# Two graph layers with attention in between: when VectorE takes statistics and squares, and when x is asked for

## Chip, cores and metric

The kernel runs on one core of a Trainium2 chip. The metric is the device time of one execution in microseconds (us); lower is better.

## What is computed

x has 16 graphs of 1024 nodes and 256 channels; adj is a sparse 1024 x 1024 matrix. Everything is 32-bit floating point. Cut to what matters:

```python
# layer 0, h = relu(layernorm(x))
c     = mean(h, channels)                        # one number per node and graph
A     = 2*abs(abs(sigmoid(c[:,None,:]-c[:,:,None]) - 0.5) - 0.5)
q     = relu((h^T @ (adj * sym(A))) * para)      # per graph, weights differ by graph
k, v  = h @ kv_w
x     = x + softmax(q k^T * scale) v             # 4 heads of 64
# layer 1, h = relu(layernorm(x)), A_hat = normalized adj, the same for all graphs
agg   = A_hat @ h                                # aggregate
y     = agg @ W1^T + b1                          # 512 columns, "hidden"
h1    = relu(batchnorm(y))                       # statistics over all graphs and nodes
out   = batchnorm(h1 @ W2^T + b2)
x     = x + out
```

The batch norm over all graphs is why the hidden results y are written to DRAM, with their statistics collected on the way, and read again in a second pass.

## The kernel before

**Layout.** A graph is held as 8 tiles of 128 nodes. The products of 1024 x 1024 with 1024 x 256 (queries and aggregate) and the hidden product use a seven-product scheme on halves, so that each has seven products whose sums are made on VectorE. All products go through three PSUM banks that rotate, `ps_mm` with the tag "mm" (`bank`, `product`, L174): a product can start when the result that lay in its bank three banks ago has been taken out.

**Two streams woven by hand.** The program's order on each engine is the order in which Python emits it. `attention` runs over 16 graphs x 16 steps. A step issues a pair of score tiles (`scores`, matmul L1056, exponential on ScalarE L1064), sums of exponentials on VectorE (L1085, L1088), and the values of the step before (L1099). Between them it takes pieces from a generator, `background(b)`, until the pieces' costs (their products' TensorE time) have caught up with what is due. So a step of attention alternates with two to five pieces of other work for neighbouring graphs. `weave(main, (start, side), ...)` takes from `start` on one piece of a side for each piece of `main`, and empties the sides at the end. `soon(action)` puts an action behind the next piece.

**The background of graph b** (from 1 on): four pieces of keys and values for b+1 with parts of the weights (`weigh`: ScalarE L506, L514, VectorE L493, adj loads L192); the queries of b+1 (`queries`, 14 pieces, VectorE L569 and L577 to L603, para loads L549); the first aht loads of the aggregate; x of b+2 (`load_x`, L186); the other keys and values with the norm of layer 1 for b-1. Then the aggregate of b-1 (`aggregate`, 14 pieces of 1.71 us of TensorE, aht loads L714, evictions L730 to L756, steps L786 to L788), and the hidden product of b-1 (`hidden`, 14 pieces of 0.86).

**Beside the aggregate** stands `summed(b+2)`: the norm of x for layer 0 (`Norm`: statistics L344 and L346 on VectorE, rsqrt on GpSimd L96/L97, L357 on VectorE, relu with row sums on ScalarE L368) in eight pieces, then `differences(b+2)`: the row sums turned (L465), written to DRAM (L467) and read back as a broadcast tile cbc (L471), which L506 needs.

**Beside the hidden product** stands `prepare(b+2)`. After two pieces it calls `squares` (two 32 x 32 block transposes of 128 x 1024 each, L438, then one write of 1 MB from GpSimd's queue, L442), and `gathered` reads the result back in another order as the transposed h (L450), which the keys need. The tile of the squares comes from the two buffers tagged "h", which x of the next graphs and the normalized h of layer 1 use too.

**The hidden product** per graph: seven products for each of two column blocks c, in the order shown in `hidden`; ten y tiles from `py` (tag "y", 6 buffers). `put` writes a finished y to DRAM (L824, GpSimd's queue) and takes its statistics (L825), one piece later: eight per graph. L831, L837, L842, L847, L851, L860 and L866 take the products out of their banks; L856 and L869 are GpSimd sums.

**Once, in the background of graph 0**: `plain_queries(1)` (16 pieces) with the norm of graph 2, `graph` (the combinations aht of the adjacency, GpSimd) and `degrees` (its row and column sums; ScalarE L241, VectorE L243/L244). `load_later` in the background of graph 1 loads W1, makes its sums on GpSimd (L309 to L312), writes dinv to DRAM (L314) and reads it back as a broadcast (L315).

SyncE's queue holds all loads, in program order; a load that waits holds up those behind it.

Of the kernel before, what the change touches and what calls it, by code (L numbers as in the profile page):

```python
# [10 lines left out]
F32 = mybir.dt.float32  # L11
# [6 lines left out]
P = 128  # L18
# [5 lines left out]
def gnn_two_layers_kernel(  # L24
# [12 lines left out]
    nc = tc.nc  # L37
# [3 lines left out]
    CC = C // P  # L41
# [57 lines left out]
    def layers(shifted):  # L99
# [10 lines left out]
        p2 = st.enter_context(tc.tile_pool(name=f"p2_{kind}", bufs=2))  # L110
        p3 = st.enter_context(tc.tile_pool(name=f"p3_{kind}", bufs=3))
        p8 = st.enter_context(tc.tile_pool(name=f"p8_{kind}", bufs=8))
        py = st.enter_context(tc.tile_pool(name=f"py_{kind}", bufs=6))

        p4 = attn.enter_context(tc.tile_pool(name=f"p4_{kind}", bufs=4, side="right"))
        ps_sc = attn.enter_context(
# [14 lines left out]
        def soon(action):  # L131

            queue.append(action)
# [298 lines left out]
        def squares(b):  # L432

            sq = p2.tile([P, CC, N], F32, tag="h", name=f"sq_{b}")
            for k in range(CC):
                nc.vector.transpose(  # L438
                    sq[:, k].rearrange("p (i t s) -> p i t s", i=NS, s=SQ),
                    hs["a", b][:, :, k * P : (k + 1) * P].rearrange("p t (i s) -> p i t s", s=SQ),  # L440
                )
            nc.gpsimd.dma_start(out=hsq_d[b], in_=sq)  # L442

        def gathered(b, k):

# [349 lines left out]
        def hidden(b):  # L795

            if b >= B - 2:
                yield from plain_hidden(b)
                return
            HH = H1 // 2  # L800
            a11, a12, _, a22 = w1_quarters()
            s1, s2, s3, s4 = (later["s"][:, i] for i in range(4))
            b11, t3, b21, b22 = at_quarters(b)
            t1, t2 = steps[b]
            t4 = p2.tile([P, FB], F32, tag="para", name=f"at4_{b}")
            nc.gpsimd.tensor_sub(t4, b21, t2)

            def left(block, c):
                return block[:, c * P : (c + 1) * P]

            def one(name, block, c, right):
                part = bank(f"py_{b}_{c}_{name}")
                product(part, left(block, c), right, True, True)
                return part

            made = {}

            def new(name, c):
                made[name] = py.tile([P, FB], F32, tag="y", name=f"y_{b}_{c}_{name}")
                return made[name]  # L820

            def put(y, n, j):
                i = b * NH + n
                nc.gpsimd.dma_start(out=y1_d[i][:, j, :], in_=y)  # L824
                soon(lambda: nc.vector.bn_stats(stats1[:, j, i, :], y))  # L825

            add = nc.vector.tensor_add

            def m1(c):
                part = one("1", a11, c, b11)  # L830
                nc.scalar.activation(  # L831
                    new("11", c), part, AF.Identity, bias=b1[:, c : c + 1]
                )

            def m2(c):
                y = made["11"]
                add(y, one("2", a12, c, b21), y)  # L837
                put(y, 0, c)

            def m3(c):  # L840
                y = made["12"]
                add(y, one("3", s4, c, b22), y)  # L842
                put(y, 1, c)

            def m4(c):
                y = made["21"]
                add(y, one("4", a22, c, t4), made["sum"])  # L847
                put(y, 0, 2 + c)

            def m5(c):  # L850
                nc.scalar.copy(new("22", c), one("5", s1, c, t1))  # L851
                if c == 1:
                    both(c)

            def both(c):
                nc.gpsimd.tensor_add(new("12", c), made["21"], made["22"])  # L856

            def m6(c):
                y = new("21", c)
                add(y, one("6", s2, c, t2), made["11"])  # L860
                if c == 0:
                    both(c)

            def m7(c):
                part, y = one("7", s3, c, t3), made["22"]
                nc.vector.scalar_tensor_tensor(  # L866
                    new("sum", c), part, b1_step[:, c : c + 1], made["21"], op0=ALU.add, op1=ALU.add
                )
                nc.gpsimd.tensor_add(y, y, made["sum"])  # L869
                put(y, 1, 2 + c)  # L870

            for c, order in ((0, (m1, m5, m6, m2, m3, m7, m4)), (1, (m1, m6, m2, m5, m7, m3, m4))):
                for each in order:
                    each(c)
                    yield 0.86

        def plain_hidden(b):

# [47 lines left out]
        def summed(b):  # L926
            yield from Norm(b, True).all()
            differences(b)
            yield 0.0

        def prepare(b, products):


            w = weighers[b]
            yield from islice(products, 1)
            yield from islice(products, 1)
            squares(b)
            yield from weave(islice(products, 5), (0, islice(w, 2)))
            gathered(b, 0)
            yield from weave(islice(products, 3), (0, islice(w, 1)))  # L940
            gathered(b, 1)
            yield from weave(islice(products, 3), (0, islice(w, AHEAD - 3)))
            yield from products
# [3 lines left out]
        def background(b):  # L947

            if b == 0:
                differences(1)  # L950
                for k in range(CC):
                    yield TOP
                    transposed(1, (k,))
                    yield 1.0
                w, products, norm = weighers[1], keys_values(1), Norm(2, True).all()
                yield from weave(islice(products, 4), (0, double(islice(w, 8))))
                yield from weave(
                    plain_queries(1), (0, w), (4, norm), (5, graph()), (7, degrees())
                )
                differences(2)  # L960
                w = weighers[2]
                yield from islice(products, 1)
                yield from weave(islice(products, 2), (0, islice(w, 2)))
                yield TOP
                transposed(2, (0,))
                yield 1.0
                yield from weave(islice(products, 1), (0, islice(w, 1)))
                yield from islice(w, 1)
                yield TOP
                transposed(2, (1,))  # L970
                yield 1.0
                yield from islice(w, AHEAD - 4)
                yield from products
                return
            before = hidden(b - 1)
            gather = aggregate(b - 1)
            if b + 1 < B:
                w, products, norm = weighers[b + 1], keys_values(b + 1), normed(b - 1)
                yield from weave(islice(products, 4), (0, islice(w, 4)))
                if b == 1:  # L980
                    load_later()
                yield from weave(queries(b + 1), (0, double(w)), (9, islice(norm, 5)))
                yield next(gather)
                if b + 2 < B:
                    load_x(b + 2, True)
                yield from weave(products, (0, norm))
            else:
                yield next(gather)
                yield from weave(endings.pop(), (2, normed(b - 1)))
            if b + 2 < B:  # L990
                yield from weave(gather, (3, summed(b + 2)))
                yield from prepare(b + 2, before)
            elif b + 2 == B:

                yield from gather
                endings.append(before)
            else:
                yield from gather
                yield from weave(before, (0, normed_last()))

        def shifted_attention(b):
# [285 lines left out]
        with st:  # L1287
            if shifted:
                for b in range(B):
                    if b > 0:  # L1290
                        load_x(b)
                    run(Norm(b, True).all())
                    differences(b)
                    for k in range(CC):
                        transposed(b, (k,))
                    run(islice(weighers[b], AHEAD))
                    run(weave(plain_queries(b), (0, weighers[b])))
                    if b == 0:
                        run(degrees(), graph())
                        load_later()  # L1300
                    run(keys_values(b))
                    shifted_attention(b)
                    norm = Norm(b, False)
                    run(norm.all())
                    keep(b)
                    if b == B - 1:
                        attn.close()
                        turns.append(second(kind))
                    run(aggregate(b), hidden(b))
            else:  # L1310
                idle = bank("idle")

# [375 lines left out]
```

## Time and profile before

| | |
|---|---|
| median of 3 runs | 2480.53 us (2480.22 to 2481.03) |
| the profiled execution | 2482.2 us, span 2480.3 us, mean granted clock 0.992 |
| TensorE matmul busy | 2418.3 us, 97% |
| VectorE busy | 1999.8 us, 81% |
| ScalarE busy | 1261.2 us, 51% |
| GpSimd busy | 565.2 us, 23% |
| period of a graph | about 135.5 us |
| L825 statistics | 112 of 687 ns |
| L438 squares | 26 of 1220 ns |

The profile names engines PE (TensorE; PEld is its weight load), DVE (VectorE), ACT (ScalarE), POOL (GpSimd) and SP (SyncE). A timeline row has the start, the duration, engine, line, operation, output and inputs, and in brackets the engine's idle time just before it with what ended it. A row of a table of stages has the stage, its length and the busy time of PE, PEld, DVE, ACT and POOL with the number of instructions, then the granted clock, the DMA share and GB/s. Since matmuls overlap in the array, busy TensorE is not TensorE at its pace: compare starts.

### The profile page before, as it was taken

To read this page: it belongs to the slowest core of one execution; us is meant where nothing else is said; L and a number is where in the kernel's file an instruction comes from. 1 tells how busy PE (TensorE), PEld (TensorE's weight loads), DVE (VectorE), ACT (ScalarE), POOL (GpSimd) and SP (SyncE) were. 2 spreads that over 40 slices of the span, in tenths; PEclk is the share of its full clock that TensorE was granted. 3 is DMA by queue.
4 is the path that set the end of the run, shared out by engine and by line. 5 is a ranking of instruction groups with operands and counts; after the bars stand their busy time and mean duration, and the time that the engine had idled before them with its cause. 6 is when DMAs were issued, how large, how long until landed. Compare 5 with 4: busy or idle time off the path is not lost. (4 is left out here: it accounts for less than half of the span.)

```text
span 2480.3 us, 35952 instructions
## 1 busy us (share of the span) xinstructions
PE 2418.3 (97%) x13290; PEld 829.3 (33%) x13290; DVE 1999.8 (81%) x3103; ACT 1261.2 (51%) x1870; POOL 565.2 (23%) x632
## 2 busy tenths in 40 slices
PE   9999999999999999999999999999999999999995
PEld 4333232332323232323323232323233232334444
DVE  5678887979798888889797978888897978767775
ACT  7764454545463645545454645355454534345554
POOL 1480202112121202021111212120201102136652
PEclk9999999999999999999999999999999999999997
DMA  4665535354555544453545555544535453456559
GB/s 145 198 218 175 181 124 191 120 198 157 181 174 191 168 168 162 144 181 118 210 143 175 170 191 170 187 160 148 177 126 197 133 199 122 157 205 222 192 198 373
DMA packets 202682, 437.19 MB, mean 176 GB/s; under 512 B 21248, under 2 KB 96512, under 8 KB 196736
## 3 DMA queue, kind: packets, MB, share of 16 engines
q1 hardware_dynamic: 173328, 327.29, 39.9%
q0 software_dynamic: 29168, 107.50, 11.4%
q8 instruction: 107, 1.75, 0.3%
q14 instruction: 79, 0.65, 0.1%
HBM read 331.36 MB, written 103.35 MB: 175 GB/s over the span
## 5 line engine op out<-in xcount | busy, mean ns | idle before, releaser
L1064 ACT ACTIVATE p<-sc 128x1024 f32<-128x1024 f32 x512 | 495.6, 1020 | 581.4 <-PE sc L1056 579.7
L1088 DVE TENSOR_TENSOR acc<-acc,p 128x1024 f32<-128x1024 f32 x384 | 469.5, 1223 | 81.6 <-ACT p L1064 60.3
L1056 PE MATMUL sc<-q,k 64*64 64x512 f32 x4096 | 500.1, 603 | 4.2 <-ACT p L1064 4.2
L1099 PE MATMUL o<-p,v 128*64 128x512 f32 x2048 | 494.6, 604 | 0.0
L174 PE MATMUL pa<-aht,h_b 128*64 128x512 f32 x1536 | 346.0, 592 | 1.1 <-ACT h_b L368 1.1
L174 PE MATMUL pg<-w,x_h 128*64 128x512 f32 x1472 | 332.0, 592 | 1.9 <-DVE x_h L579 1.9
L1056 PEld LDWEIGHTS sc<-q,k 64*64 64x64 f32 x4096 | 131.7, 132 | 340.9 <-issue 287.8
L1117 POOL DMA_DIRECT2D out_d<-os x58 | 33.9, 584 | 914.9 <-DVE os L1113 883.9
L1099 PEld LDWEIGHTS o<-p,v 128*64 128x64 f32 x2048 | 124.4, 136 | 297.9 <-issue 272.4
L493 DVE SCALAR_TENSOR_TENSOR w<-w,adj 128x1024 f32<-128x1024 f32 x128 | 166.2, 1306 | 31.9 <-ACT w L514 26.1
L174 PEld LDWEIGHTS pa<-aht,h_b 128*64 128x64 f32 x1536 | 110.0, 137 | 220.7 <-issue 208.8
L174 PEld LDWEIGHTS pg<-w,x_h 128*64 128x64 f32 x1472 | 105.6, 137 | 212.4 <-issue 201.0
L506 ACT ACTIVATE w<-cbc,csum 128x512 f32<-128x512 f32 x256 | 170.3, 716 | 4.7 <-DMA cbc<-csum_d 4.7
L514 ACT ACTIVATE w<-w 128x1024 f32<-128x1024 f32 x128 | 135.5, 1059 | 2.5
L569 DVE TENSOR_TENSOR w<-w,w 128x1024 f32<-128x1024 f32 x112 | 133.2, 1219 | 1.5
L174 PE MATMUL py<-at,w1s 128*64 128x512 f32 x448 | 109.5, 598 | 9.7 <-DVE y L837 7.5
L174 PE MATMUL pv<-kvw_f,ht 128*64 128x256 f32 x1024 | 116.1, 379 | 0.0
L174 PE MATMUL pk<-ht,kvw_f 128*64 128x512 f32 x512 | 115.2, 592 | 0.2 <-ACT ht L430 0.2
L174 PE MATMUL py<-at,w 128*64 128x512 f32 x464 | 113.3, 595 | 1.3 <-DVE at L727 0.7
L368 ACT ACTIVATE x_h<-x_h,lnsm_a 128x256 f32<-128x256 f32 x120 | 70.5, 593 | 74.6 <-DMA aht<-aht_d 67.1
L1085 DVE TENSOR_TENSOR acc<-p,p 128x1024 f32<-128x1024 f32 x64 | 79.2, 1237 | 31.5 <-ACT p L1064 31.5
L1428 ACT ACTIVATE yin_f<-yin_f,sm_f 128x512 f32<-128x512 f32 x128 | 93.5, 802 | 15.0 <-DMA yin_f<-y_d 14.9
(197 smaller groups left out, 2967.1 us busy)
## 6 DMA issues: line engine op xcount, KB each, us to landing
aht<-aht_d SPq DMA_DIRECT2D x224, 512.0 KB
adj<-in_adj_dram SPq DMA_DIRECT2D x128, 512.0 KB
y_d<-y POOLq DMA_DIRECT2D x128, 256.0 KB, 3.8
yin_f<-y_d SPq DMA_DIRECT2D x32, 1024.0 KB
para<-in_para_dram SPq DMA_DIRECT2D x64, 256.0 KB
x_d<-x_x POOLq DMA_DIRECT2D x16, 1024.0 KB, 5.1
xo_f<-x_d SPq DMA_DIRECT2D x32, 512.0 KB
out_dram<-xo_f POOLq DMA_DIRECT2D x32, 512.0 KB, 11.1
```

The source lines that it names most:

```text
L174: nc.tensor.matmul(dst[r], left[:, r], right, start=start, stop=stop)
L368: nc.scalar.activation(self.h[:, t, :], self.src[:, t, :], AF.Relu, bias=self.sm[:, 1, t : t + 1], scale=self.sm[:, 0, t : t + 1], accum_o ...
L493: nc.vector.scalar_tensor_tensor(w, w, 1.0, a, op0=ALU.add, op1=ALU.mult)
L506: nc.scalar.activation(w[:, t, :].rearrange("p (t q) -> p t q", q=P), cbc[:, q * NT // NH : (q + 1) * NT // NH], AF.Abs, bias=csum[:, th * ...
L514: nc.scalar.activation(made[i], made[i], AF.Tanh, scale=-0.5 / C)
L569: nc.vector.tensor_sub(block(i)[part], block(x)[part], block(y)[part])
L1056: nc.tensor.matmul(sc[part, e, :], ks[b][k][r, m * P + c * HW : m * P + (c + 1) * HW], qs[b][k][r, f * FB : (f + 1) * FB], start=True, sto ...
L1064: nc.scalar.activation(pr, sc, AF.Exp)
L1085: nc.vector.tensor_add(self.acc, self.held, pr)
L1088: nc.vector.tensor_add(self.acc, self.acc, pr)
L1099: nc.tensor.matmul(self.o[r, :], vs[b][k][:, m, r], pr[:, e, :], start=(m == 0), stop=(m == NT - 1),)
L1428: nc.scalar.activation(y, y, AF.Relu, bias=sh[:, j : j + 1], scale=scale[:, j : j + 1])
```

## The change

Eight edits. (1) `py` gets 7 buffers. (2) `squares` becomes a generator that writes each half to a 4 KB tile of its own (a pool with one buffer) and sends each half off by itself, with three pieces between; it runs at the end of `summed`, so within the aggregate. (3) `summed` starts with the aggregate's first piece instead of its fourth. (4) Of the eight statistics per graph, five go to a list, `late`, and are taken from the second piece of the next graph's aggregate on, one per piece; the other three come two pieces after their result instead of one. (5) x of b+2 is asked for ahead of the first aht loads. (6) In the background of graph 0 `differences(2)` comes after 13 of 16 pieces of the queries; the rest of `graph` and `degrees` goes beside the last three. (7) `load_later` comes after seven pieces of the queries, with all adj loads of that graph emitted before. (8) `gathered` and the weights in `prepare` stand a piece earlier or later.

```diff
-        py = st.enter_context(tc.tile_pool(name=f"py_{kind}", bufs=6))
+        py = st.enter_context(tc.tile_pool(name=f"py_{kind}", bufs=7))
...
-            sq = p2.tile([P, CC, N], F32, tag="h", name=f"sq_{b}")
             for k in range(CC):
+                sq = p1.tile([P, N], F32, tag="sq", name=f"sq_{b}_{k}")
                 nc.vector.transpose(
...
-            nc.gpsimd.dma_start(out=hsq_d[b], in_=sq)
+                nc.gpsimd.dma_start(out=hsq_d[b][:, k], in_=sq)
+                for _ in range(3):
+                    yield 0.0
...
-            def put(y, n, j):
+            def put(y, n, j, deferred):
                 i = b * NH + n
                 nc.gpsimd.dma_start(out=y1_d[i][:, j, :], in_=y)
-                soon(lambda: nc.vector.bn_stats(stats1[:, j, i, :], y))
+
+                def stats():
+                    nc.vector.bn_stats(stats1[:, j, i, :], y)
+
+                if deferred:
+                    late.append(stats)
+                else:
+                    soon(lambda: soon(stats))
...
-                put(y, 0, c)
+                put(y, 0, c, c == 1)
...
-                put(y, 1, c)
+                put(y, 1, c, True)
...
-                put(y, 0, 2 + c)
+                put(y, 0, 2 + c, c == 1)
...
-                put(y, 1, 2 + c)
+                put(y, 1, 2 + c, c == 1)
...
+        late = []
+
+        def lately():
+
+            while late:
+                late.pop(0)()
+                yield 0.0
...
             differences(b)
             yield 0.0
+            yield from squares(b)
...
-            squares(b)
-            yield from weave(islice(products, 5), (0, islice(w, 2)))
             gathered(b, 0)
+            yield from weave(islice(products, 6), (0, islice(w, 2)))
...
+                asked, build, sums = plain_queries(1), graph(), degrees()
                 yield from weave(
-                    plain_queries(1), (0, w), (4, norm), (5, graph()), (7, degrees())
+                    islice(asked, 13),
+                    (0, w),
+                    (4, norm),
+                    (5, islice(build, 8)),
+                    (7, islice(sums, 6)),
                 )
                 differences(2)
+                yield from weave(asked, (0, build), (0, sums))
...
+                asked = queries(b + 1)
+                yield from weave(islice(asked, 7), (0, double(w)))
                 if b == 1:
                     load_later()
-                yield from weave(queries(b + 1), (0, double(w)), (9, islice(norm, 5)))
-                yield next(gather)
+                yield from weave(asked, (2, islice(norm, 5)))
                 if b + 2 < B:
                     load_x(b + 2, True)
+                yield next(gather)
...
-                yield from weave(gather, (3, summed(b + 2)))
+                yield from weave(gather, (0, summed(b + 2)), (1, lately()))
...
-                yield from gather
+                yield from weave(gather, (1, lately()))
```

More of the change, by code (lines that the diff above doesn't have):

```diff
@@ L432, in squares @@
         def squares(b):
-            sq = p2.tile([P, CC, N], F32, tag="h", name=f"sq_{b}")
             for k in range(CC):
+                sq = p1.tile([P, N], F32, tag="sq", name=f"sq_{b}_{k}")
                 nc.vector.transpose(
-                    sq[:, k].rearrange("p (i t s) -> p i t s", i=NS, s=SQ),
+                    sq.rearrange("p (i t s) -> p i t s", i=NS, s=SQ),
                     hs["a", b][:, :, k * P : (k + 1) * P].rearrange("p t (i s) -> p i t s", s=SQ),
                 )
-            nc.gpsimd.dma_start(out=hsq_d[b], in_=sq)
+                nc.gpsimd.dma_start(out=hsq_d[b][:, k], in_=sq)
+                for _ in range(3):
+                    yield 0.0
         def gathered(b, k):
@@ L990, in background @@
             if b + 2 < B:
-                yield from weave(gather, (3, summed(b + 2)))
+                yield from weave(gather, (0, summed(b + 2)), (1, lately()))
                 yield from prepare(b + 2, before)
             elif b + 2 == B:
-                yield from gather
+                yield from weave(gather, (1, lately()))
                 endings.append(before)
             else:
-                yield from gather
+                yield from weave(gather, (1, lately()))
                 yield from weave(before, (0, normed_last()))
@@ L1308, in layers @@
                         turns.append(second(kind))
-                    run(aggregate(b), hidden(b))
+                    run(aggregate(b), hidden(b), lately())
             else:
```

## The prediction

> **What bounds the kernel now.** I read the page's busy table first, then the two stages that the change touches, with TensorE's own rows beside VectorE's, and last the one-off gaps of the first graphs.
>
> ```profile
> PE 2418.3 (97%) x13290; PEld 829.3 (33%) x13290; DVE 1999.8 (81%) x3103; ACT 1261.2 (51%) x1870; POOL 565.2 (23%) x632
> ```
>
> TensorE is the bound nearly everywhere, so only time in which it misses its own pace can be won. Its pace shows in the rows of one second projection (graph period 135.5 us, this one at 690 to 710 us). Eight records are four starts of a concurrent pair, 0.43 us apart, so the next row should start 1.72 us later.
>
> ```profile
> 697.06 1.89 PE L174 MATMUL py<-at,w1s 128*64 128x512 f32 x8
> 698.77 1.93 PE L174 MATMUL py<-at,w 128*64 128x512 f32 x8
> 700.87 1.08 PE L174 MATMUL py<-at,w1s 128*64 128x512 f32 x4 [0.17 <-DVE y_sum L866]
> ...
> 706.50 1.89 PE L174 MATMUL py<-at,w1s 128*64 128x512 f32 x8
> 708.96 1.08 PE L174 MATMUL py<-at,w1s 128*64 128x512 f32 x4 [0.57 <-DVE y L837]
> ```
>
> 697.06 to 698.77 keeps pace; 700.87 is 0.38 late and 708.96 is 0.74 late. The idle in brackets is 0.17 smaller, because a matmul's modelled end (0.60) lies 0.17 behind the next regular start. Both wait for a PSUM bank that VectorE empties late, and VectorE's rows say why:
>
> ```profile
> 698.88 0.68 DVE L842 TENSOR_TENSOR y<-py,y 128x512 f32<-128x512 f32 x1
> 699.49 0.68 DVE L825 BATCH_NORM_STATS2 stats<-y 128x6 f32<-128x512 f32 x1
> 700.09 0.73 DVE L866 SCALAR_TENSOR_TENSOR y_sum<-py,vec,y 128x512 f32<-128x512 f32 x1
> ...
> 705.81 2.49 DVE L1088 TENSOR_TENSOR acc<-acc,p 128x1024 f32<-128x1024 f32 x2
> 708.22 0.69 DVE L837 TENSOR_TENSOR y<-py,y 128x512 f32<-128x512 f32 x1
> ```
>
> A statistic stands between two evictions, and no row has idle time before it. By stage (aggregate, projection):
>
> ```profile
> 645.00:690.00 45.00, 45.00 (x254) 14.00 (x252) 34.29 (x62) 16.44 (x29) 5.98 (x8) 1.00 0.47 162
> 690.00:714.00 24.00, 23.26 (x132) 6.60 (x130) 22.59 (x31) 15.00 (x19) 10.97 (x12) 1.00 0.78 249
> ```
>
> The third busy column is VectorE: 34.29 of 45 in the aggregate, 22.59 of 24 in the projection. The waits of TensorE count 13 of each kind, one per graph 0 to 12.
>
> Two gaps come once. In the first, the exponentials of the attention stand in ScalarE's queue behind a weight waiting for the broadcast sums:
>
> ```profile
> 146.41 1.94 PE L1099 MATMUL o<-p,v 128*64 128x512 f32 x8
> 152.05 3.40 PE L1056 MATMUL sc<-q,k 64*64 64x512 f32 x16 [3.71 <-ACT p L1064]
> ```
> ```profile
> 148.26 1.33 ACT L506 ACTIVATE w<-cbc,csum 128x512 f32<-128x512 f32 x2 [4.70 <-DMA cbc<-csum_d]
> ```
>
> In the second, SyncE's queue stops at L314/L315 (dinv and its broadcast), the adj loads L192 behind it start late, and VectorE stops at L493:
>
> ```profile
> 188.03 0.34 SPq L315 DMA_DIRECT2D dbc_f<-dinv_d  x1
> 188.42 0.43 SPq L549 DMA_DIRECT2D para<-in_para_dram  x1
> 188.95 2.05 SPq L192 DMA_DIRECT2D adj<-in_adj_dram  x2
> ```
> ```profile
> 195.92 1.89 PE L174 MATMUL pg<-w,s_a 128*64 128x512 f32 x8
> 199.75 1.94 PE L174 MATMUL pg<-w,x_h 128*64 128x512 f32 x8 [1.95 <-DVE x_h L579]
> ```
>
> [...] L493 takes 1.21 us at 702.88 but 1.93 at 710.20, beside a GpSimd add of 2.14; so I move no such pair for free. [...] for the 1 MB of squares, where the trace shows 5.0.
>
> **The change, part by part.**
>
> *Squares and five statistics leave the projection.* The projection sheds 2 x 1.22 (L438) and 5 x 0.69 (L825) = 5.9 us of VectorE per graph. I replay VectorE's queue by row durations, TensorE at its pace. Without the squares, L842 runs when its product is done, at 698.13 instead of 698.88. The remaining statistic of product 2 comes two pieces later, so L866 starts when its product is done, 698.98, ends 699.71, and its bank is wanted at 700.49: the 0.38 goes. Then L825, L847, L825 (waits for GpSimd L869 until 701.1), L860, L493, L825 and the group sums lead to the two L1088 at 704.65, and L837 runs 707.05 to 707.74. Its bank is wanted at 707.87 (708.22 less the first stall): the 0.74 goes, with only about 0.1 us in hand. Value: 13 x 1.12 = 14.6 us; for the thin margin I charge 0.1 x 13 = 1.3, net 13.3. Bounds: 14.6, and 13 x 0.7 = 9 if half of the second stays.
>
> *The same 5.9 us enter the aggregate*, with the norm's statistics three pieces sooner. 34.29 + 5.9 = 40.2 of 45 us, so it fits on average; the places count. Replaying: L734 ends at 659.3 (was 658.5), L755 about 669.9 (was 667.2) with its bank wanted at 672.09, L744 691.2 (was 690.8) with its bank wanted at 691.60. VectorE stops about 0.5 us twice at L357 for GpSimd's rsqrt (0.57 + 1.04), included. The p buffers of one step are freed at 669.3 and wanted at 678.55. So TensorE loses nothing: cost 0; cover 2.1, 0.4 and 9 us. If it falls, each us beyond costs 13 us.
>
> *The squares' new tile, two DMAs, py 7.* One more GpSimd issue, 0.56 us, in a stage where GpSimd is busy 5.98 of 45 us. The second transpose (685.5) must wait until the first half has left: issue at 678.4 plus [...] the measured 5.0: 683.4. Behind a longer wait would stand L1134 and L744. The gathers L450 no longer wait (113 us in SyncE's queue in total), but the first products with ht come at 714.47, so nothing is won there. Ten y tiles per graph go round in seven buffers, and the tile reused seven later is always one whose statistic was not kept: cost 0.
>
> *x sooner.* SyncE issues x at 634.2 instead of 638.24, ahead of five aht loads. These come 1 us later at issue and, by 1 MB at the 370 GB/s seen there, about 2.9 us later in data: first one near 640, wanted at 647.0. Cost 0, cover 7 us. x itself is in by about 638, and the first norm statistic now stands at 649.5: no wait.
>
> *Sums of graph 2 three pieces sooner.* L465 moves from 137.02 to about 125.9; cbc took 11.2 us from there to use, so it is in by 137.1, and ScalarE wants it at 143.6. Behind the L467/L471 waits in SyncE's queue stands one adj_t load, about 5 us later, for ScalarE's L241 at 132.4: at most 2 to 3 us for ScalarE there, before a TensorE row that needs it. Won: 152.05 less 148.17 is 3.9, and the scores row takes 3.33 until the next start instead of 1.88 (144.53 to 146.41): 1.5. Together 5.4; bounds 3 to 5.4.
>
> *load_later behind the adj loads.* The two adj loads no longer stand behind L315. 199.75 less 197.64: 2.1 won. GpSimd's four w1s sums (1.1 to 1.7 us each) move to about 195 to 203 and may stretch L569 beside them (1.22 to 1.57): bounds 0 to 2.1.
>
> Sum: 13.3 + 5.4 + 2.1 = 20.8; less 0.3 for the w1s sums, 20.5. The profiled execution took 2482.2 us (span 2480.3), 1.7 above the median of 2480.53; the gains are stalls within the span, so they come off either: 2480.5 - 20.5 = 2460.0. All bounds at their best: 14.6 + 5.4 + 2.1 = 22.1, 2458.4.
>
> **The rivals.**
> A: the second stall of the projection stays in part. For it: only 0.1 us in hand, and VectorE still busy throughout. 0.3 to 0.6 x 13 = 4 to 8 us kept: about 2465. Chance 0.16.
> B: the one-off gaps only move (ScalarE late at 132 us, L569 stretched at 200 us), the projection gains: 2480.5 - 13.3 = 2467. Against it: 6 us in hand at 143.6. Chance 0.11.
> C, slower: VectorE falls behind in the aggregate, at L755. In-order, it stops at L357 for GpSimd's rsqrt and at the second transpose for the DMA, and evictions queue behind it. It costs from 2.1 us beyond my replay and turns the whole into a loss at 2.1 + 21.8/13 = 3.8. At 5 us, 2.9 x 13 = 38 less 21.8 gives +16: 2496. Against it: 4.8 us of VectorE idle time are still left in this stage. Chance 0.07.
> D: the deferral only moves the stall, gain and loss cancel: 2480. Chance 0.03. That the edits don't take effect is excluded, as they are plain program order.
>
> **How the numbers follow.** The forecast's own range is 2458 to 2463, chance 0.63. A measurement tells some 0.2% (5 us) from no change. Faster: forecast, A and B, 0.90; same 0.03; slower 0.07. For 8 in 10 the range takes the best bound with half a us, 2458, and reaches over A and B to 2467.5; left out are C, D and edges, some 0.13.
>
> **What would show it.** Right: no wait of py for L837 or L866; L825 five times per graph in the aggregate; sc after 146 us at pace; L493 near 190 without a wait for adj; aggregates still at 45.0 of 45 us. Wrong: a wait of pa for L734, L755 or L744 (C), of the second L438 for its DMA, or of py for L837 near 708 (A).

## Result and the profile after

| | before | after |
|---|---|---|
| median, compared on one chip (4 runs each) | 2480.78 us (2480.22 to 2484.66) | 2460.35 us (2460.19 to 2460.42) |
| ratio of the runs | | 0.9914, 95% interval 0.9897 to 0.9931 |
| span of the profiled execution | 2480.3 us | 2458.6 us |
| graph period, graphs 3 to 13 | 135.47 us | 134.39 us |
| period of graph 0 / 1 / 2 | 110.75 / 138.80 / 136.20 | 105.52 / 135.56 / 134.40 |
| graph 14 to the end | 550.25 us | 550.66 us |

The kernel became 0.86% faster, and the interval lies clear of 1. A period is counted here from a graph's first score matmul to the next graph's. The periods account for the whole difference: 5.23 + 3.24 + 1.80 from the first three, 11 x 1.08 = 11.9 from graphs 3 to 13, 0.4 given back in the end part: 21.7 us of span (2480.3 to 2458.6).

Graph 2 gained 1.80 us, 0.72 more than the later ones. It had a third stall, which the prediction's sum leaves out (TensorE's timeline of the kernel before, in the hidden product of graph 1):

```profile
427.10 1.03 PE L174 MATMUL py<-at,w 128*64 128x512 f32 x4
428.67 1.08 PE L174 MATMUL py<-at,w 128*64 128x512 f32 x4 [0.55 <-DVE y L842]
```

The second row should start 0.86 us after the first and starts after 1.57. After the change no such wait is left.

The page's row for TensorE after:

```profile
PE 2412.4 (98%) x13290; PEld 832.6 (34%) x13290; DVE 2003.9 (82%) x3103; ACT 1257.7 (51%) x1870; POOL 559.5 (23%) x645
```

The work is the same (13290 matmuls, 3103 VectorE instructions); GpSimd has 13 more issues, one more write of squares per graph. The same projection as in the prediction, TensorE's timeline after:

```profile
685.67 1.89 PE L174 MATMUL py<-at,w1s 128*64 128x512 f32 x8
687.38 1.89 PE L174 MATMUL py<-at,w 128*64 128x512 f32 x8
689.10 1.03 PE L174 MATMUL py<-at,w1s 128*64 128x512 f32 x4
...
693.82 1.03 PE L174 MATMUL py<-at,w 128*64 128x512 f32 x4
694.68 2.90 PE L174 MATMUL py<-at,w1s 128*64 128x512 f32 x12
697.41 1.03 PE L174 MATMUL py<-at,w 128*64 128x512 f32 x4
```

685.67, 687.38, 689.10: 1.72 us apart, at pace. 694.68 to 697.41 is 2.73 for twelve records, which at pace take 2.57: 0.16 of the second stall is left (0.11 of waiting and 0.05 at the restart, of which more below). VectorE's timeline of the same stretch (the lines are numbered anew: L842, L866, L825 and L837 are now L851, L875, L829 and L846):

```profile
686.81 0.69 DVE L851 TENSOR_TENSOR y<-py,y 128x512 f32<-128x512 f32 x1
687.60 0.75 DVE L875 SCALAR_TENSOR_TENSOR y_sum<-py,vec,y 128x512 f32<-128x512 f32 x1
688.27 0.69 DVE L829 BATCH_NORM_STATS2 stats<-y 128x6 f32<-128x512 f32 x1
...
695.76 0.69 DVE L846 TENSOR_TENSOR y<-py,y 128x512 f32<-128x512 f32 x1
```

L851 now starts 0.12 us after its product's last matmul ends (686.69, the fourth of the eight records), where it was 0.80 before, and no statistic stands between it and L875. The stages, moved with TensorE (aggregate, projection):

```profile
633.60:678.60 45.00, 45.00 (x254) 14.01 (x252) 38.88 (x69) 16.33 (x29) 6.74 (x10) 1.00 0.62 214
678.60:702.60 24.00, 24.00 (x138) 7.24 (x136) 20.94 (x29) 14.90 (x19) 10.72 (x13) 1.00 0.47 162
```

VectorE went from 34.29 to 38.88 in the aggregate and from 22.59 to 20.94 in the projection. The windows cut its queue at other instructions than before, since it runs earlier or later against TensorE, so the differences are not 5.9; the direction and the 24.00 of 24.00 of TensorE in the projection are what to read (the 0.11 of waiting that is left does not show there, as matmuls overlap by 0.17).

The first one-off gap, TensorE after (before: 146.41, then 152.05):

```profile
146.36 1.94 PE L1124 MATMUL o<-p,v 128*64 128x512 f32 x8
148.23 1.95 PE L1081 MATMUL sc<-q,k 64*64 64x512 f32 x16
```

The second, SyncE's queue after: adj leaves before dinv and its broadcast.

```profile
170.44 7.42 SPq L192 DMA_DIRECT2D adj<-in_adj_dram  x2
...
179.09 0.46 SPq L314 DMA_DIRECT2D dinv_d<-deg  x1
189.76 0.34 SPq L315 DMA_DIRECT2D dbc_f<-dinv_d  x1
```

TensorE's queries go on at pace, 1.72 us apart, and VectorE no longer waits for adj there:

```profile
190.64 1.89 PE L174 MATMUL pg<-w,s_a 128*64 128x512 f32 x8
192.36 1.89 PE L174 MATMUL pg<-w,x_h 128*64 128x512 f32 x8
```

### The profile page after: what moved, and what is told of

Same layout as the page of the kernel before. It is cut to its first block, busy times and chain, and to the rows that moved or that the text cites. A ratio compares the mean times of both kernels' runs of the same rounds, so it can differ in the third digit from the quotient of the medians.

```text
span 2458.6 us, 35932 instructions
## 1 busy us (share of the span) xinstructions
PE 2412.4 (98%) x13290; PEld 832.6 (34%) x13290; DVE 2003.9 (82%) x3103; ACT 1257.7 (51%) x1870; POOL 559.5 (23%) x645
## 3 DMA queue, kind: packets, MB, share of 16 engines
q8 instruction: 107, 1.75, 0.3%
## 5 line engine op out<-in xcount | busy, mean ns | idle before, releaser
L826 POOL DMA_DIRECT2D y_d<-y x112 | 61.6, 550 | 145.1 <-DVE y L846 75.8
L1160 DVE TENSOR_REDUCE part<-acc 128x16 f32<-128x512 f32 x128 | 87.8, 686 | 4.4
## 6 DMA issues: line engine op xcount, KB each, us to landing
out_dram<-xo_f POOLq DMA_DIRECT2D x32, 512.0 KB, 11.1
```

The source lines that it names most:

```text
L1160: nc.vector.tensor_reduce(self.part[:, e, :], acc.rearrange("p (c s) -> p c s", s=SQ), AX.X, ALU.add)
```

## The experiments

They ran on three chips, and on each the kernel before was run again beside them, 20 to 31 times. Its times lie between 2477.6 and 2487.2 us, medians 2483.6, 2482.8 and 2483.4: wider and higher than in the first runs. The last point of the part on the prediction returns to that; the graph periods of the profiled executions, nearly all of which repeat to 0.02 us within a run, are given beside the times. Periods are those of graphs 3 to 13.

| run | period, us | graphs 0 / 1 | median, us | ratio to before (95%) |
|---|---|---|---|---|
| order only | 135.11 | 106.77 / 142.19 | 2479.18 | 0.9983 (0.9974 to 0.9991) |
| statistics only | 134.77 | 106.88 / 144.19 | 2474.97 | 0.9965 (0.9951 to 0.9979) |
| squares only | 134.78 | 110.37 / 140.18 | 2475.12 | 0.9965 (0.9952 to 0.9977) |
| one-off edits only | 135.47 | 105.52 / 136.62 | 2474.51 | 0.9963 (0.9949 to 0.9978) |
| row sums sooner only | 135.47 | 105.52 / 145.14 | 2481.91 | 0.9996 (0.9987 to 1.0005) |
| load_later later only | 135.47 | 110.44 / 136.63 | 2479.36 | 0.9981 (0.9974 to 0.9988) |
| change, aht first | 134.39 | 105.53 / 135.58 | 2459.97 | 0.9905 (0.9887 to 0.9924) |
| change, kept statistics twice | 134.39 | 105.52 / 135.57 | 2460.07 | 0.9906 (0.9887 to 0.9924) |
| change, kept statistics thrice | 136.54 | 105.53 / 135.57 | 2488.00 | 1.0021 (1.0014 to 1.0028) |

### Order only

```diff
-                soon(lambda: nc.vector.bn_stats(stats1[:, j, i, :], y))
+                soon(lambda: soon(lambda: nc.vector.bn_stats(stats1[:, j, i, :], y)))
```

> The kernel before, with one edit: each statistic of a hidden result comes two pieces after the result instead of one; none is kept for later, the squares stay. Theory (both stalls of the projection are VectorE's queue, the first by order, the second by load): the statistic no longer stands between L842 and L866, so the first stall (0.34 us of the period) goes, and the second (0.74) stays, as the same work lies ahead of L837. Period 135.47 to about 135.1 us, time about 2476 (-4.5). Rival (only the load counts): no change, 2480.5. Rival (order alone is enough): period 134.4, 2466.5.

Period 135.11, as expected: the first stall is a matter of order alone. The second stays (TensorE's timeline of this run):

```profile
698.11 1.93 PE L174 MATMUL py<-at,w 128*64 128x512 f32 x8
699.86 1.03 PE L174 MATMUL py<-at,w1s 128*64 128x512 f32 x4
...
705.44 1.89 PE L174 MATMUL py<-at,w1s 128*64 128x512 f32 x8
707.93 1.08 PE L174 MATMUL py<-at,w1s 128*64 128x512 f32 x4 [0.60 <-DVE y L837]
```

699.86 is 0.03 late, where it had been 0.38. 705.44 + 1.72 = 707.16, so 707.93 is 0.77 late, where it had been 0.74. Both rivals fall.

### Statistics only, squares only

The first has edits 1 and 4 of the change, the second 2, 3, 5 and 8, each on the kernel before. Edits 1 and 8 were not run by themselves. One line of each diff:

```diff
-                yield from weave(gather, (3, summed(b + 2)))
+                yield from weave(gather, (3, summed(b + 2)), (1, lately()))
```
```diff
-                yield from weave(gather, (3, summed(b + 2)))
+                yield from weave(gather, (0, summed(b + 2)))
```

> The kernel before, with only the statistics' edits: seven y buffers, five of eight statistics kept for the next aggregate, the other three two pieces later; squares, x and the one-off edits as before. Theory: the first stall goes; by the same replay L837 starts at 707.55 and ends at 708.2, its bank is wanted at 707.87, so about 0.4 of the second stall's 0.74 stays. Period about 134.8 us, time about 2471.5 (-9). Rival (the statistics are all of it): period 134.4, 2466.5. Rival (the squares are the cause): period above 135.2.

> The kernel before, with the squares within the aggregate, the norm's statistics from its first piece and x asked for ahead of aht; all eight statistics one piece after their result, as before. Theory: without 2.4 us of squares L842 and L866 come 0.7 us sooner and the first stall goes; L837 starts at 707.4 and ends at 708.1, so about 0.3 of the second stall stays. Period about 134.7 us, time about 2470.5 (-10). So this half alone and the statistics alone each give most of the gain, and their sum is more than both together give. Rival (the two halves cure one stall each): period 135.1 here or with the statistics alone.

Periods 134.77 and 134.78. Of the second stall each leaves part (TensorE with statistics only, then with squares only; L844 and L839 are their L837):

```profile
706.11 1.89 PE L174 MATMUL py<-at,w1s 128*64 128x512 f32 x8
708.27 1.08 PE L174 MATMUL py<-at,w1s 128*64 128x512 f32 x4 [0.27 <-DVE y L844]
```
```profile
705.19 1.89 PE L174 MATMUL py<-at,w1s 128*64 128x512 f32 x8
707.39 1.08 PE L174 MATMUL py<-at,w1s 128*64 128x512 f32 x4 [0.32 <-DVE y L839]
```

0.44 and 0.48 late, where the replay had said 0.4 and 0.3. Each half alone wins 0.70 us per graph, both together 1.08 and not 1.40: the first stall is cured by either (its row comes after 1.75 and 1.72 us), the second takes the load of both. The third stall of graph 2 goes with the squares (its period is 134.78 there, 135.50 with statistics only, 135.83 with order only). The rivals, one cause for each or one for all, fall.

### The two one-off edits, together and apart

Edits 6 and 7 on the kernel before, then each by itself.

> The kernel before, with only the two one-off edits: the row sums of graph 2 are sent off after 13 of 16 pieces, and W1, dinv and their broadcast come after the adj loads. Theory: the two gaps go, 5.4 and 2.1 us, and nothing else changes: the first period 110.75 to about 105.4, the second 138.8 to about 136.7, the others 135.47; time about 2473 (-7.5). Rival (the gaps only move to a later load or to the GpSimd sums): 2478 to 2480.5.

Periods of graphs 0 and 1 as expected (105.52, 136.62), the others unchanged. In time it was worth 2483.57 - 2474.51 = 9.1 us, interval 5 to 13; by the two periods it is 5.2 + 2.2 = 7.4. But in the runs with order or statistics only, the first gap had turned out short (106.8) and the second long (142 and 144), without an edit near either. That raised the question whether the gaps are two.

> The kernel before, with one edit: the row sums of graph 2 are sent off after 13 of 16 pieces. Theory formed after the runs so far (the two gaps hang together: the second ends at an adj load behind L315, whose time is set by the graph sums on GpSimd and the slow write of dinv, not by TensorE): the first gap goes (first period 105.5), but TensorE reaches the second 5 us sooner and waits there longer, second period 142 to 145; time about as before, within 3 us. Theory of the prediction (the gaps are independent): first period 105.4, second still 138.8, 5.4 us less than before.

> The kernel before, with one edit: W1, dinv and their broadcast come after the adj loads of graph 2. Theory (gaps that hang together): the second gap goes whatever the first is: second period 136.6; the first stays and varies with when cbc lands, first period 106 to 111; time about 2475 to 2480, some 4 us under the kernel before. Theory of the prediction: first 110.75, second 136.7, 2478.4.

They hang together. With the row sums sooner the first gap goes, and the second takes it all: 145.14 for graph 1, no difference in time. TensorE's timeline and SyncE's queue of that run:

```profile
191.19 1.89 PE L174 MATMUL pg<-w,s_a 128*64 128x512 f32 x8
199.69 3.62 PE L174 MATMUL pg<-w,x_h 128*64 128x512 f32 x8 [6.61 <-DVE x_h L579]
```
```profile
177.32 0.37 SPq L314 DMA_DIRECT2D dinv_d<-deg  x1
186.63 0.34 SPq L315 DMA_DIRECT2D dbc_f<-dinv_d  x1
```

L315 goes out at 186.63 although TensorE is 5 us ahead (188.03 in the kernel before): its time comes from the graph sums on GpSimd, whose last one (L97) ends at 177.29 here and 177.62 in the kernel before and lets L314 go, and from the write of dinv, 9.3 us from L314 to L315. TensorE only starts to wait for it sooner. With `load_later` later alone the second gap is gone and the first stays. So edit 6 is worth nothing without edit 7, and 4.9 us with it (110.44 to 105.52 in the first period, at the same second one).

The length of the gaps is not only waiting. The table of stages of the row-sums run, in the gap, after it, and later:

```profile
192.90:196.40 3.50, 0.18 (x2) 0.00 (x0) 0.01 (x1) 0.00 (x0) 0.00 (x0) 0.98 0.89 334
196.40:199.70 3.30, 0.01 (x2) 0.04 (x2) 3.27 (x5) 0.00 (x0) 0.00 (x0) 0.50 0.03 12
199.70:203.20 3.50, 3.50 (x8) 0.82 (x8) 3.33 (x7) 0.63 (x1) 0.00 (x0) 0.51 0.18 51
203.30:206.00 2.70, 2.70 (x23) 1.07 (x24) 2.70 (x4) 1.60 (x2) 0.00 (x0) 1.00 0.05 20
```

The third column from the right is the granted clock: 0.50 and 0.51, from inside the gap until 3.5 us after it, and the eight records at 199.69 take 3.62 instead of 1.89. The kernel before has 0.50 in the 3.4 us from 151.6 on, at the end of its gap of 3.7 us, and 1.00 after that of 2.0:

```profile
151.60:155.00 3.40, 2.95 (x16) 0.80 (x16) 2.87 (x3) 2.21 (x3) 2.37 (x3) 0.50 0.69 246
199.70:203.00 3.30, 3.25 (x24) 1.09 (x24) 3.23 (x6) 0.85 (x2) 0.00 (x0) 1.00 0.17 32
```

With squares only the second gap is 2.35 us, and the clock after it is 0.50 (TensorE's timeline, and the stage from the gap's end on):

```profile
199.72 3.60 PE L174 MATMUL pg<-w,x_h 128*64 128x512 f32 x8 [2.35 <-DVE x_h L581]
```
```profile
199.70:203.10 3.40, 3.38 (x8) 0.85 (x8) 3.23 (x6) 0.63 (x1) 0.00 (x0) 0.50 0.24 46
```

So after 2.35 us of idle time the clock was 0.50, after 2.0 it was 1.00. What sets this, and how much the place of a gap counts, was not tried. The stretch at half clock cost about 1.5 us in the kernel before (3.33 instead of 1.88 from the scores row to the next start) and 1.7 in the row-sums run (3.55 instead of 1.87).

### x behind aht again

```diff
+                yield next(gather)
                 if b + 2 < B:
                     load_x(b + 2, True)
-                yield next(gather)
```

> The changed kernel with one edit taken back: the first five aht loads stand ahead of x in SyncE's queue, as before. Theory (cover is ample): x is asked for about 4 us later and is in by some 4 us before the first norm statistic, so VectorE does not wait; 2460.3, period 134.4. Rival (x sooner is needed for the early norm): VectorE stops at the first statistic for x, its evictions come late, period 134.6 to 136, time 2463 to 2480.

Period 134.39, 2459.97 us: the same. x left at 625.34 instead of 622.80, and nothing waited for it. This edit is worth nothing here, and the rival falls: the early norm does not need it.

### The kept statistics twice and thrice

These kernels take the same statistics of the kept results two and three times, the same values again.

```diff
-                    late.append(stats)
+                    late.extend([lambda: [stats() for _ in range(2)]])
```

> The changed kernel, with each of the five kept statistics taken twice in the aggregate (3.4 us more of VectorE per graph, the same values again). Theory (the aggregate has cover for what was moved there): four of the five stand ahead of the eviction L757, which ends at 657.5 in the trace and moves by 2.7 to 660.2; its bank is wanted at 660.70, so no stall: period 134.4, time 2460.3 to 2461. Rival (the aggregate is already at its limit): every added us shows, 3.4 x 13 = 44, about 2504.

> The changed kernel, with each kept statistic taken three times (6.9 us more of VectorE per graph). Theory: L757 moves by 5.5 to 663.0, 2.3 us after its bank is wanted: a stall of about 2.3 us per graph, period about 136.7, time about 2490. This is the point from which the deferral would have lost, so it prices the rival of the prediction that ended slower. Rival (limit already reached): 2550. Rival (cover much wider than the replay says): 2460.3.

Twice costs nothing: in the aggregate of 45.00 us VectorE is busy for 42.12 and TensorE does not wait. Thrice ends slower than the kernel before. TensorE's and VectorE's timelines of the latter:

```profile
663.79 1.92 PE L1124 MATMUL o<-p,v 128*64 128x512 f32 x8
667.09 3.65 PE L174 MATMUL pa<-aht,s_b 128*64 128x512 f32 x16 [1.38 <-DVE at L757]
```
```profile
666.35 0.69 DVE L757 TENSOR_TENSOR at<-pa,at 128x512 f32<-128x512 f32 x1
```

L757 (L755 before the change) ends at 667.04 and TensorE starts at 667.09, in the place that the prediction had named. The stall is 1.55 there and 0.49 at L746 in the same graph, 2.14 on the period with the restarts; expected were 2.3. It comes in 12 periods, graphs 2 to 13, as the aggregate of graph 0 has no kept statistics to take: 12 x 2.14 = 25.7 of the 27.7 us between the two spans (2458.6 and 2486.3). The other 2.0 are elsewhere: 0.6 before the first period, 0.6 in two longer periods, 0.9 behind graph 13.

## Why the prediction was right, by its own steps

- **Squares and statistics leave the projection**: 13.3 us forecast, 13 x 1.08 = 14.0 measured. L842 was to start at 698.13 and L837 to end 0.1 before its bank was wanted. Counted from the start of that group of products (697.06 there, 685.67 after), L842's successor starts 1.14 in, where 1.07 was forecast, and L846 10.09 in, where 9.99 was. Two small errors of the sum offset each other in part. Each stall also delays the next start by 0.05, so the two were worth 1.22 per graph and not 1.12. And the margin of 0.1 was not there: L846 ends 10.78 in, 0.1 later than forecast, and its bank is wanted 10.73 in instead of 10.81. 0.16 stayed, where 0.1 was charged.
- **The third stall**, 0.7 us in graph 2, is in none of its terms, though its wait stood in the trace. It went too.
- **Rival A** (part of the second stall stays) is those 0.16, less than its 0.3 to 0.6; with one half of the change alone it would have been 0.44 to 0.48.
- **The aggregate takes the work at no cost**: right. The kernel with the statistics twice shows a further 3.4 us of cover, the one with thrice where it ends. The replay's L755, 2.1 us ahead of its need, was 3.2 ahead: its successor L757 ends at 657.51 and TensorE wants the bank at 660.70. The wait at L357 is not the reason, as it took 0.89 of the 1.0 us charged (at 650.42); which other term was too large stays open.
- **Rival C** had put its start 2.1 us and the loss of the whole at 3.8 us beyond the replay (3.7 with the forecast's own gain of 20.5); 3.4 us more of work cost nothing and 6.9 lost the whole, so mechanism and place were right, and the point lies between.
- **x sooner at no cost**: right; and without a gain.
- **The one-off gaps**: 5.4 and 2.1 less 0.3 forecast, 7.2. From the two profiled executions graphs 0 and 1 gained 5.23 + 3.24, of which 1.08 is the projection's: 7.4. Right in sum, wrong in reasoning in one point: the step took the gaps as independent. Row sums alone win nothing. That the sum came out is luck to that extent: both edits were in the change. Rival B, that the gaps only move, is true of that edit alone and not of the two together. And the 1.5 us that the scores row took too long, which the step only counted, are the halved clock (0.50 from 151.6 to 155.0). The 0.3 charged for the w1s sums did not come (with edits 6 and 7 alone the second period loses 2.18), and ScalarE's wait at L241, forecast at 2 to 3 us at most, took 3.08, with no start of TensorE behind it.
- **The level.** 2460.0 was forecast, 2460.35 measured. That they lie so close is in part luck. The gain in span was 21.7 where 20.5 was forecast (0.7 more in the projection, 0.7 from the third stall, 0.2 at the one-off gaps, 0.4 lost at the end), and the median of three from which the forecast was taken, 2480.53, lay 1.7 below the profiled execution; the two misses nearly cancel. The gain against the first runs of before was 20.4 us; against the median of 23 later ones, 2482.78, it is 22.4. The times of kernels with a gap left scatter (before: 10 us; row sums alone: 9; load_later alone: 6), those without it hardly (0.2 us after the change, 1.1 with the one-off edits alone, 1.1 in 20 runs with the kept statistics thrice). Which wait, or which stretch at half clock, varies from one execution to the next was not measured and stays open.

## What to carry to other kernels

When one engine empties another's buffers in order, ask of each instruction in its queue whether somebody waits for what stands behind it; a result that only the end needs can be kept, if buffers reach, for a stage in which the queue has idle time, and how much more that stage takes is found by doubling the moved work. Two gaps that end at different waits can be one: before one is priced, see what sets the time of the next wait downstream. Replay the queue by durations, not by busy shares, and read late starts from the pace, not from the idle time shown.

## What the runs showed of the hardware

- **A write in 4-byte packets landed late.** dinv is 4 KB, written as 1024 packets of 4 bytes (of 1104 packets under 512 bytes between L314 and L315). In the kernel before its last packet is done 3.7 us after L314 (181.4), no packet of any queue follows, and L315, which waits for the write, goes out at 188.03: 6.6 us in which the transfer engines moved nothing. After the change the same lag is 5.7 (184.05 to 189.76). From L314 to L315 it took 10.4 us in the kernel before and 10.7 after the change, and between 9.3 (statistics only) and 11.1 (one-off edits only) in five of the experiments. The csum write (L467), of the same size in packets of 128 bytes, is four issues, and in the kernel before the load that waits for it follows 0.9 to 2.5 us after the last, in most graphs 1.0. That the size of the packets is the cause was not tried.
- **Half clock after a gap**, as above: 3.4 us at 0.50 with a gap of 3.7 us (kernel before) and with one of 2.35 (squares only), 1.00 after one of 2.0 (kernel before).
- **A restart cost 0.05 us** more than the wait: in the kernel before, after the second stall in the projection the next start came 0.91 us later instead of 0.86 (708.96 to 709.87), after the first 1.01 instead of 0.96.
